# A two-layer graph network on one core: a head start for the second layer, its root term added early, and other groups at the end

## The chip, the cores and the metric

The kernel runs on one core of a Trainium2 chip. The metric is the device time of one execution in microseconds. Twenty executions of the kernel before had a median of 4745.5 us, from 4725.66 to 4767.5. One execution was profiled; it took 4727.98 us.

## The reference

There are N = 12500 nodes with C = 128 channels, and E = 200000 edges that are sorted by destination. Every edge has 42 attributes; the greatest of ten of them gives its relation. Two layers of a relational graph convolution follow, then a residual and a normalisation, all in 32-bit floating point:

```python
seg = dst * NUM_REL + edge_type
xs = x[src]
sums = jax.ops.segment_sum(xs, seg, num_segments=N * NUM_REL)
cnt = jax.ops.segment_sum(jnp.ones(seg.shape, x.dtype), seg, num_segments=N * NUM_REL)
mean = (sums / jnp.maximum(cnt, 1.0)[:, None]).reshape(N, NUM_REL, -1)
return jnp.einsum('nrd,rdo->no', mean, w_rel) + x @ root + bias
...
edge_type = jnp.argmax(msg[:, NODE_EMB_DIM:-NODE_EMB_DIM], axis=1).astype(jnp.int32)
h = jax.nn.relu(_rgcn_layer(x, src, dst, edge_type, w_rel1, root1, b1))
return _rgcn_layer(h, src, dst, edge_type, w_rel2, root2, b2)
...
x = _layernorm(x + _L0_gnn_ref(...), axis=-1)
```

So a layer needs, for each edge, the row of its source node; for each node, ten means over its incoming edges, each times its own 128 x 128 matrix; and the node's own row times a root matrix, plus a bias.

## The kernel before, in words

The edges are cut into 1563 tiles of 128 edges, and the tiles into groups: 95 groups of 16 tiles and then small ones, 8, 8, 8, 8, 4, 4 and 3 tiles. Both layers run over the groups in this order. The edges of a group lie within a short stretch of nodes, since they are sorted.

For each group these steps follow one another, and the steps of neighbouring groups overlap:

- POOL gathers the source rows of each tile with an indirect DMA (line 466) into one of three buffers g, from x in layer 1 and from hD, the hidden nodes in DRAM, in layer 2. One wait covers a whole group.
- DVE builds for each tile a matrix oh (line 481): an edge's weight (one over its count) in the column of its relation and its node's place among twelve.
- PE multiplies rows and oh into zp, sums by relation and node (line 495). There is one zp of four PSUM banks.
- ACT copies zp to zs (line 509), PE multiplies by the relations' matrices into pp (line 521), ACT copies to ms (line 527), PE spreads the result over 160 node columns with a placement matrix at (line 537), and DVE adds these to acc at an offset read from a register (line 543). acc has one column per node, and lies in SBUF for the whole time.

The weights of the edges need the relation and the counts of 13 chunks of 128 tiles (types() and count()). Chunk c+1 is prepared in steps while layer 1 runs over chunk c: the list todo holds, for each chunk, the group by which its steps are to be done and how many there are, and layer() runs some steps after each group.

A node block is finished as soon as no later group can touch it. There are 29 blocks: 23 of 512 nodes, five of 128 and one of 84. done_after() tells the tile after which a block is finished: blocks 23 to 28 fall into the small groups at the end. For a block, block_in() loads its rows of x (layer 2: also of hD), transposes the rows on PE (line 407) and copies them to fT (line 409). block_rows() adds the bias to the block's columns of acc (line 416), clears these columns in layer 1 (line 418), and multiplies fT by the root matrix and a by the identity into one PSUM tile (lines 421 and 422). In layer 1 hidden() applies relu (line 435) and stores the rows to hD. In layer 2 final() adds x (line 447), normalises (lines 450 to 457) and stores the rows to the output. The PSUM pool ps_f with its two buffers serves these steps and the counting.

Layer 2's first gather waits for all stores to hD. All direct DMAs of blocks and chunks are issued from SP. The order of instructions on an engine is given by a scheduler that works from the program order and its own estimates, except where keep_in_program_order fixes it.

After layer 2 a branch follows that is taken only where the data breaks an assumption of the fast path (a node with very many edges, for example); with these inputs it isn't taken.

Of the kernel before, what the change touches and what calls it, by code (L numbers as in the profile page):

```python
# [9 lines left out]
F32 = mybir.dt.float32  # L10
BF16 = mybir.dt.bfloat16
I32 = mybir.dt.int32
# [31 lines left out]
def rgcn_resnorm_kernel(ctx: ExitStack, tc: tile.TileContext, x, src, dst, attr, w_rel1, root1, b1,  # L44
# [25 lines left out]
    while t < NT:  # L70
        groups.append((t, min(HT if NT - t > 3 * QB else QB, NT - t)))
        t += groups[-1][1]
# [15 lines left out]

    HALF = NT * P - E
    assert C == P and E % GT == 0 and 0 < HALF < P and NT % CT and 1 < groups[-1][1] < groups[-2][1]  # L90

# [26 lines left out]
    wE = keep.tile([P, NCH * CT], F32, name="wE")  # L118

# [46 lines left out]

    def sources(c):
        p = chunk_rows(c)
        s_i = prep.tile([P, P], I32, name="s_i")
        rows_from(s_i, src, c, 0, P)  # L170
        s_f = prep.tile([P, P], F32, name="s_f")
        early(c, nc.vector.tensor_copy(s_f[:p], s_i[:p]))
        return to_edges(idxE, s_f, c)
# [112 lines left out]
    def types(c):  # L286
# [3 lines left out]
        d_i = prep.tile([P, P + L + 1], I32, name="d_i")  # L290
        if last:
            nc.vector.tensor_copy(d_i[:p, P:], pads[:p])
            q = p - 1
            nc.sync.dma_start(d_i[:q], bass.AP(dst.tensor, dst.offset + c * CE, [[P, q], [1, P + L + 1]]))
            nc.sync.dma_start(d_i[q:p, :P], bass.AP(dst.tensor, dst.offset + E - P, [[P, 1], [1, P]]))
        else:
            rows_from(d_i, dst, c, 0, P + L + 1)
        n = p - 1 if last else p
        ty = prep.tile([P, P], F32, name="ty")
        H = P // 2  # L300
        for o in (0, H):
            m = prep.tile([P, H * D], F32, name=f"m{o // H}")
            d = nc.sync.dma_start(m[:n], bass.AP(attr.tensor, attr.offset + (c * CE + o) * D, [[P * D, n], [1, H * D]]))
            if last:
                nc.sync.dma_start(m[n:p], bass.AP(attr.tensor, attr.offset + (E - P + o) * D,
                                                  [[P * D, 1], [1, H * D]]))
            if c == 1:
                later(d)
            argmax(c, ty[:p, o:o + H], m[:p].rearrange("p (j d) -> p j d", d=D)[:, :, EMB:EMB + NREL], p, H, prep,
                   riotaP, topP[o // H])  # L310
            yield
# [71 lines left out]
    def rows_dma(sb, dr, k, store):  # L383
        n0, n, _ = block(k)
        full = n // P
        pairs = []
        if full:
            pairs.append((sb[:, :full], dr[n0:n0 + full * P, :].rearrange("(t p) c -> p t c", p=P)))
        if n % P:
            pairs.append((sb[:n % P, full], dr[n0 + full * P:n0 + n, :]))  # L390
        for a, b in pairs:
            then("SP", nc.sync.dma_start(b, a) if store else nc.sync.dma_start(a, b))

    def block_in(k, l):

        n0, n, subs = block(k)
        last = "e" if k == NBLK - 1 else ""
        b = len(subs) if last else 4
        xb = fin.tile([P, b, C], F32, name="xb" + last)
        rows_dma(xb, x, k, False)  # L400
        fb = xb
        if l:
            fb = fin.tile([P, b, C], F32, name="hb" + last)
            rows_dma(fb, hD, k, False)
        pt = ps_f.tile([P, YB], F32, name="pf")
        for t, h in subs:
            nc.tensor.transpose(pt[:, t * P:t * P + h], fb[:h, t, :], ident[:h, :h])  # L407
        fT = fin.tile([P, b * P], F32, name="fT" + last)
        nc.scalar.activation(fT[:, :n], pt[:, :n], AF.Copy)  # L409
        return xb, fT  # L410

    def block_rows(fT, k, l):

        n0, n, subs = block(k)
        a = fin.tile([P, YB], F32, name="a")
        nc.vector.tensor_scalar(a[:, :n], acc[:, n0:n0 + n], bsb[l], None, op0=ALU.add)
        if l == 0:
            nc.vector.memset(acc[:, n0:n0 + n], 0.0)
        pr = ps_f.tile([P, 4, C], F32, name="pf")
        for t, h in subs:  # L420
            nc.tensor.matmul(pr[:h, t, :], fT[:, t * P:t * P + h], rsb[l], start=True, stop=False)  # L421
            nc.tensor.matmul(pr[:h, t, :], a[:, t * P:t * P + h], ident, start=False, stop=True)  # L422
        return pr
# [5 lines left out]
    def hidden(k, ready):  # L429

        xb, fT = ready
        pr = block_rows(fT, k, 0)
        hb = fin.tile([P, 4, C], F32, name="hb")
        for p, s in spans(k):
            nc.scalar.activation(hb[:p, s], pr[:p, s], AF.Relu)
        rows_dma(hb, hD, k, True)

    def final(k, ready):

        xb, fT = ready  # L440
        pr = block_rows(fT, k, 1)
        v = fin.tile([P, 4, C], F32, name="v")
        mv = small.tile([P, 4, 2], F32, name="mv")
        rstd = small.tile([P, 4], F32, name="rstd")
        _, n, subs = block(k)
        for p, s in spans(k):
            nc.vector.tensor_tensor(v[:p, s], pr[:p, s], xb[:p, s], op=ALU.add)  # L447
# [7 lines left out]
        o = fin.tile([P, 4, C], F32, name="o")  # L455
# [3 lines left out]
        rows_dma(o, out, k, True)  # L459
# [3 lines left out]

    def gather(table, t0, n):
        g = gpool.tile([P, G, C], F32, name="g")
        return g, [then("POOL", nc.gpsimd.indirect_dma_start(  # L466
            out=g[:, j, :], out_offset=None, in_=table, in_offset=bass.IndirectOffsetOnAxis(
                ap=idxE[:, t0 + j:t0 + j + 1], axis=0))) for j in range(n)]
# [6 lines left out]
    def ones(k):  # L475

        t0, n = groups[k]
        oh = dpool.tile([P, G, KW], F32, name="oh")
        for j in range(n):
            t = t0 + j  # L480
            then("DVE", nc.vector.tensor_scalar(oh[:, j, :], iotaP[:, :KW], keyE[:, t:t + 1], wE[:, t:t + 1],  # L481
                                                op0=ALU.is_equal, op1=ALU.mult))
# [3 lines left out]
        return oh, at  # L486

    def sums(table, k, oh, at):
# [4 lines left out]
        zp = ps_z.tile([P, G // QB, YB], F32, name="zp")  # L493
        for j in range(n) if end else reversed(range(n)):
            m = nc.tensor.matmul(zp[:, j // QB, j % QB * KW:(j % QB + 1) * KW], g[:, j, :], oh[:, j, :],  # L495
                                 start=True, stop=True)
# [48 lines left out]
    def layer(table, l, finish, steps, flag_too=False):  # L545
# [8 lines left out]
        def add_oldest():  # L554
# [3 lines left out]
            while done < NBLK and sum(groups[k]) >= done_after(done):  # L558
                finish(done, ready if done == NBLK - 1 else given or block_in(done, l))
# [3 lines left out]
        for k in range(NG):  # L563
            end = k >= NS
            if k and not given and done < NBLK - 1:
                given = block_in(done, l)
            if projected:
                add_oldest()
            if end:
# [4 lines left out]
                if not ready:  # L574
                    ready = block_in(NBLK - 1, l)
# [6 lines left out]
            held.append(sums(table, k, *(made or ones(k))))  # L582
            made = ones(k + 1) if end and k < NG - 1 else None
# [27 lines left out]
    zero = fin.tile([P, YB], F32, name="a")  # L611
    nc.vector.memset(zero, 0.0)
    for a in range(0, NPAD, YB):
        m = min(NPAD - a, YB)
        nc.scalar.activation(acc[:, a:a + m], zero[:, :m], AF.Copy)
# [3 lines left out]
    weights_in()  # L619
    todo = []  # L620
    for c in range(1, NCH):
        s = [as_steps(sources, c + 1)] if c + 1 < NCH else []
        todo.append((c * CT // G - 2, [8 + L // DB + 2], chain(*s, types(c), count(c))))
# [22 lines left out]

    gp = ctx.enter_context(tc.tile_pool(name="gp", bufs=2))
# [120 lines left out]
    with tc.If(flag > 0):  # L768
# [3 lines left out]
        for l, (table, finish) in enumerate(((x, hidden), (hD, final))):  # L772
            nc.vector.memset(acc, 0.0)
# [29 lines left out]
```

## Time and profile before

| | |
|---|---|
| median of 20 executions | 4745.5 us (4725.66 to 4767.5) |
| the profiled execution | 4727.98 us |
| its span, first to last instruction | 4726.2 us |
| granted TensorE clock in it | 0.746 |
| busy: POOL, PE, DVE, ACT | 63%, 58%, 32%, 11% of the span |
| start-up, until the first add to acc | 0 to 99 us |
| full groups of layer 1 | until 2284.6 us |
| small groups of layer 1 | until 2389.3 us |
| full groups of layer 2 | until 4617.5 us |
| small groups of layer 2 | until 4726.2 us |

A row of the timeline begins with the start in us and the length in us. After the operation stand the tiles, as output<-input, the shapes and the number of instructions that the row joins; in brackets the engine's idle time before it and what ended that. In the page's groups the columns after the bar are the busy time, the mean of one instruction in ns, and the idle time before them with its releaser. PE does each matmul of 32-bit numbers in two records. In the table by stage each engine's busy time and number of instructions are followed by the granted clock, the share of the DMA engines and GB/s.

### The profile page before, as it was taken

What the parts mean: (1) busy time and instruction counts of PE and PEld (TensorE: products, weight loads), DVE (VectorE), ACT (ScalarE), POOL (GpSimd) and SP (SyncE); (2) the same over time, 40 slices, a digit from 0 to 9 for tenths busy, and PEclk for the clock granted to TensorE, in tenths of its full rate; (3) what the DMA queues carried; (4) which work ended last, traced back from release to release, by engine and by line L of the source; (5) the groups of instructions that cost most, each with busy time, mean ns of one, the idle gap of its engine ahead of it and who ended that gap; (6) DMA issues with size and microseconds to landing.
All of it is one profiled execution on the core that took longest, in us unless ns stands there. A gap on an engine that the chain in (4) does not pass through costs nothing.

```text
span 4726.2 us, 43799 instructions
## 1 busy us (share of the span) xinstructions
PE 2759.9 (58%) x16206; PEld 2528.9 (54%) x16206; DVE 1511.0 (32%) x4660; ACT 530.9 (11%) x1142; POOL 2964.5 (63%) x3142
## 2 busy tenths in 40 slices
PE   2656566656656565655636556555556565665557
PEld 2545555555555555555625555555555555555556
DVE  4243333333334333333222322222222222222223
ACT  1010111111111111111101111111111111111111
POOL 5666666666666666666556666666666666666663
PEclk7777777777777777777766777777777777777778
DMA  4122222122122221211111111111111111111111
GB/s 132 48 72 79 62 63 80 49 76 74 55 76 62 63 77 49 57 49 49 45 48 48 55 52 52 56 55 52 52 56 55 52 50 57 54 52 52 57 53 39
DMA packets 180538, 278.99 MB, mean 59 GB/s; under 512 B 55608, under 2 KB 127175, under 8 KB 177191
## 3 DMA queue, kind: packets, MB, share of 16 engines
q0 software_dynamic: 100032, 205.07, 15.2%
q1 hardware_dynamic: 78577, 71.03, 4.7%
q8 instruction: 132, 2.16, 0.2%
q14 instruction: 89, 0.73, 0.0%
q10 hardware_dynamic: 1708, 0.01, 0.0%
HBM read 262.28 MB, written 13.60 MB: 58 GB/s over the span
## 4 chain that ended last, share of the span: by engine, by line
PE 36%; another core or an unknown queue 30%; issue 22%; DVE 10%; ACT 1%; DMA 0%; DVEq 0%; ACTq 0%
PE pp L521 17%; PE zp L495 12%; DVE oh L481 6%; PE pp L537 3%; PE pf L422 2%; PE pf L421 1%; ACT zs L509 1%; DVE at L485 1%; DVE acc L543 1%; PE pf L366 0%; PE pf L364 0%; PE pf L407 0%; DVE eqb L362 0%; DVE st L450 0%
## 5 line engine op out<-in xcount | busy, mean ns | idle before, releaser
L466 POOL DMA_INDIRECT g<-in_x_dram,idxE x1563 | 1481.2, 948 | 886.2 <-issue 428.3
L466 POOL DMA_INDIRECT g<-hD,idxE x1563 | 1480.6, 947 | 851.0 <-issue 453.3
L521 PE MATMUL pp<-w,zs 128*96 128x128 f32 x7880 | 1346.5, 336 | 702.1 <-issue 565.2
L521 PEld LDWEIGHTS pp<-w,zs 128*96 128x96 f32 x7880 | 1231.5, 212 | 823.8 <-issue 677.9
L495 PE MATMUL zp<-oh,g 128*128 128x120 f32 x6252 | 1030.9, 323 | 304.6 <-issue 267.3
L481 DVE TENSOR_SCALAR oh<-bank,keyE,wE 128x120 f32<-128x120 f32 x3126 | 1003.0, 391 | 570.4 <-remote 471.9
L495 PEld LDWEIGHTS zp<-oh,g 128*128 128x128 f32 x6252 | 981.0, 239 | 321.4 <-issue 299.0
L543 DVE TENSOR_TENSOR acc<-acc,pp 128x160 f32 x204 | 65.7, 322 | 1834.7 <-remote 1440.4
L509 ACT ACTIVATE zs<-zp 128x480 f32<-128x480 f32 (+1 forms) x782 | 385.6, 574 | 2172.6 <-remote 1606.6
L537 PE MATMUL pp<-at,ms 96*128 96x160 f32 (+1 forms) x788 | 208.1, 398 | 656.3 <-issue 545.9
L537 PEld LDWEIGHTS pp<-at,ms 96*128 96x128 f32 (+1 forms) x788 | 149.0, 241 | 699.7 <-issue 579.1
L527 ACT ACTIVATE ms<-pp 96x256 f32<-96x256 f32 (+1 forms) x198 | 74.5, 376 | 1310.7 <-remote 995.3
L422 PE MATMUL pf<-ident,a 128*128 128x128 f32 x392 | 116.8, 389 | 148.6 <-issue 73.6
L422 PEld LDWEIGHTS pf<-ident,a 128*128 128x128 f32 x392 | 90.7, 282 | 161.9 <-issue 81.5
L421 PE MATMUL pf<-root,fT 128*128 128x128 f32 x388 | 107.2, 366 | 70.0 <-issue 55.0
L362 DVE TENSOR_TENSOR eqb<-pf,kh 128x1344 bf16<-128x1344 f32 (+2 forms) x65 | 100.3, 1550 | 134.7 <-PE pp L537 74.4
L485 DVE TENSOR_SCALAR at<-bank,place 96x160 f32<-96x160 f32 x394 | 133.0, 371 | 0.0
L421 PEld LDWEIGHTS pf<-root,fT 128*128 128x128 f32 x388 | 86.7, 271 | 71.8 <-issue 55.4
L447 DVE TENSOR_TENSOR v<-pf,xb 128x512 f32<-128x512 f32 (+1 forms) x28 | 17.4, 620 | 219.4 <-remote 161.1
L369 DVE TENSOR_REDUCE wp<-pf 128x128 f32<-128x512 f32 (+2 forms) x13 | 9.0, 691 | 170.0 <-remote 155.2
L364 PE MATMUL pf<-eqb,identb 128*128 128x512 bf16 (+2 forms) x130 | 53.1, 409 | 15.7 <-DVE eqb L362 9.9
L409 ACT ACTIVATE fT<-pf 128x512 f32<-128x512 f32 (+1 forms) x56 | 30.3, 541 | 284.8 <-remote 239.7
(107 smaller groups left out, 484.4 us busy)
## 6 DMA issues: line engine op xcount, KB each, us to landing
m<-in_edge_attr_dram SPq DMA_DIRECT2D x24, 1344.0 KB
g<-in_x_dram,idxE POOLq DMA_INDIRECT x1563
g<-hD,idxE POOLq DMA_INDIRECT x1563
xb<-in_x_dram SPq DMA_DIRECT2D x46, 256.0 KB
hD<-hb SPq DMA_DIRECT2D x23, 256.0 KB
hb<-hD SPq DMA_DIRECT2D x23, 256.0 KB
out_dram<-o SPq DMA_DIRECT2D x23, 256.0 KB
w<-in_L_gnn_w_rel_dram SPq DMA_DIRECT2D x2, 640.0 KB
```

Source lines behind the costliest of these rows:

```text
L362: nc.vector.tensor_tensor(eq[:p], kp[:p, None, :R].to_broadcast([p, DB, R]), fore, op=ALU.is_equal)
L421: nc.tensor.matmul(pr[:h, t, :], fT[:, t * P:t * P + h], rsb[l], start=True, stop=False)
L422: nc.tensor.matmul(pr[:h, t, :], a[:, t * P:t * P + h], ident, start=False, stop=True)
L466: return g, [then("POOL", nc.gpsimd.indirect_dma_start(out=g[:, j, :], out_offset=None, in_=table, in_offset=bass.IndirectOffsetOnAxis(ap= ...
L481: then("DVE", nc.vector.tensor_scalar(oh[:, j, :], iotaP[:, :KW], keyE[:, t:t + 1], wE[:, t:t + 1], op0=ALU.is_equal, op1=ALU.mult))
L485: nc.vector.tensor_scalar(at[:, h, :], iotaP[:HR], place[:, h, k:k + 1], None, op0=ALU.is_equal)
L495: m = nc.tensor.matmul(zp[:, j // QB, j % QB * KW:(j % QB + 1) * KW], g[:, j, :], oh[:, j, :], start=True, stop=True)
L509: then("ACT", nc.scalar.activation(zs[:, :, b * QB:b * QB + m, :], zp[:, b, :m * KW].rearrange("c (j r n) -> c r j n", r=NREL, n=WN), AF.C ...
L521: nc.tensor.matmul(po[:m * WN, h], zs[:, r, h * HT:h * HT + m].rearrange("c j n -> c (j n)"), wsb[l][:, r, :], start=(r == 0), stop=(r == ...
L527: nc.scalar.activation(ms[:, :n // HT], po[:HR, :n // HT], AF.Copy)
L537: nc.tensor.matmul(pa, ms[:m * WN, h], at[:m * WN, h], start=(h == 0), stop=(h == len(parts) - 1))
L543: nc.vector.tensor_tensor(acc[:, s], acc[:, s], pa, op=ALU.add)
```

## The change

- **Groups.** The small groups at the end are 8, 8, 8, 12 and 7 tiles in place of 8, 8, 8, 8, 4, 4 and 3.
- **A head for layer 2.** The first 16 tiles of layer 2 gather from the first 12288 rows of hD alone, with indices held below 12288 (idxH). Edges whose source is one of the last 212 nodes get weight zero there (wH). Their part is added by late_sums(): matmuls of late_h, the rows of the last two blocks as they lie in SBUF, and late_w, which says for each of the last 212 nodes with what weight it goes to which column. head() builds late_w in five steps during the last full groups of layer 1, with a matmul per tile and block. The last chunk's preparation is to be done four groups earlier.
- **No nodes loaded in layer 2.** acc starts from layer 1's bias, set by ACT after the weights have come. hidden() transposes its rows in SBUF after relu, multiplies them by layer 2's root matrix (one matmul of up to 512 columns), and writes that, plus layer 2's bias, plus fT (the transposed rows of x) over the block's columns of acc. So final() only transposes acc into PSUM and normalises from there; block_in() does nothing in layer 2.
- **Shared transfers.** Sources and destinations of four chunks come in one DMA each; the attributes of a chunk in one instead of two; rows of x, hD and the output for two blocks of 512 nodes in one.

```diff
-        groups.append((t, min(HT if NT - t > 3 * QB else QB, NT - t)))
+        n = NT - t
+        groups.append((t, HT if n > 2 * HT + QB else HT + QB if n > HT + QB else n))
...
+    EARLY = starts[NBLK - 2]
...
+    def of_four(c, a, name, n):
+
+        if c == 0 or c == NCH - 1:
+            return prep.tile([P, n], I32, name=name)
+        if c % 4 == 1:
+            q = min(4, NCH - 1 - c)
+            four[name] = prep.tile([P, 4, n], I32, name=name + "4")
+            nc.sync.dma_start(four[name][:, :q], bass.AP(a.tensor, a.offset + c * CE, [[P, P], [CE, q], [1, n]]))
+        return four[name][:, (c - 1) % 4]
...
+        m = prep.tile([P, P * D], F32, name="m")
         for o in (0, H):
-            m = prep.tile([P, H * D], F32, name=f"m{o // H}")
-            d = nc.sync.dma_start(m[:n], bass.AP(attr.tensor, attr.offset + (c * CE + o) * D, [[P * D, n], [1, H * D]]))
...
+            w = H if c == 0 else P
+            if w == H or not o:
+                d = nc.sync.dma_start(m[:n, o * D:(o + w) * D], bass.AP(
+                    attr.tensor, attr.offset + (c * CE + o) * D, [[P * D, n], [1, w * D]]))
...
     def block_in(k, l):
 
+        if l:
+            return None
...
-        a = fin.tile([P, YB], F32, name="a")
-        nc.vector.tensor_scalar(a[:, :n], acc[:, n0:n0 + n], bsb[l], None, op0=ALU.add)
-        if l == 0:
-            nc.vector.memset(acc[:, n0:n0 + n], 0.0)
...
+    def hidden(k, fT):
+
+        n0, n, subs = block(k)
+        pr = ps_f.tile([P, 4, C], F32, name="pf")
+        for t, h in subs:
+            nc.tensor.matmul(pr[:h, t, :], fT[:, t * P:t * P + h], rsb[0], start=True, stop=False)
+            nc.tensor.matmul(pr[:h, t, :], acc[:, n0 + t * P:n0 + t * P + h], ident, start=False, stop=True)
+        i = k - (NBLK - 2)
+        hb = late_h[:, i:i + 1] if i >= 0 and not anew else half(k, "hb")
         for p, s in spans(k):
             nc.scalar.activation(hb[:p, s], pr[:p, s], AF.Relu)
-        rows_dma(hb, hD, k, True)
...
+        rows_dma(hb, hD, k, True, "hb")
+        pt = ps_f.tile([P, YB], F32, name="pf")
+        for t, h in subs:
+            nc.tensor.transpose(pt[:, t * P:t * P + h], hb[:h, t, :], ident[:h, :h])
+        hT = fin.tile([P, YB], F32, name="hT")
+        nc.scalar.activation(hT[:, :n], pt[:, :n], AF.Copy)
+        po = ps_f.tile([P, YB], F32, name="pf")
+        nc.tensor.matmul(po[:, :n], rsb[1], hT[:, :n], start=True, stop=True)
+        nc.vector.scalar_tensor_tensor(acc[:, n0:n0 + n], po[:, :n], bsb[1], fT[:, :n], op0=ALU.add, op1=ALU.add)
+
+    def final(k, _):
+
+        n0, n, subs = block(k)
+        v = ps_f.tile([P, 4, C], F32, name="pf")
...
+        for t, h in subs:
+            nc.tensor.matmul(v[:h, t, :], acc[:, n0 + t * P:n0 + t * P + h], ident, start=True, stop=True)
...
+    def head():
+
+        nc.vector.tensor_scalar(idxH, idxE[:, :G], EARLY - 1, None, op0=ALU.min)
...
+        for b in range(0, G, QB):
+            pm = [ps_f.tile([P, YB], F32, name="pf") for _ in range(2)]
+            for j in range(QB):
+                t = b + j
+                oh = prep.tile([P, KW], F32, name="ohH")
+                nc.vector.tensor_scalar(oh, iotaP[:, :KW], keyE[:, t:t + 1], wE[:, t:t + 1],
+                                        op0=ALU.is_equal, op1=ALU.mult)
+                for i in range(2):
+                    of = prep.tile([P, P], F32, name=f"of{i}")
+                    nc.vector.tensor_scalar(of, iotaP[:, :P], off[:, i, t:t + 1], None, op0=ALU.is_equal)
+                    nc.tensor.matmul(pm[i][:, j * KW:(j + 1) * KW], of, oh, start=True, stop=True)
+            for i in range(2):
+                nc.scalar.activation(late_w[i][:, b * KW:(b + QB) * KW], pm[i][:, :QB * KW], AF.Copy)
+            yield
...
+    def late_sums(table, t0, banks):
+
+        if is_head(table, t0):
+            for b, z in enumerate(banks):
+                for i in range(2):
+                    n = block(NBLK - 2 + i)[1]
+                    nc.tensor.matmul(z[:, :QB * KW], late_h[:n, i, :], late_w[i][:n, b * QB * KW:(b + 1) * QB * KW],
+                                     start=(i == 0), stop=False)
...
-    for a in range(0, NPAD, YB):
-        m = min(NPAD - a, YB)
-        nc.scalar.activation(acc[:, a:a + m], zero[:, :m], AF.Copy)
     places()
     for _ in chain(types(0), count(0)):
         pass
     weights_in()
+    for a in range(0, NPAD, YB):
+        m = min(NPAD - a, YB)
+        nc.scalar.activation(acc[:, a:a + m], zero[:, :m], AF.Identity, bias=bsb[0])
...
-        todo.append((c * CT // G - 2, [8 + L // DB + 2], chain(*s, types(c), count(c))))
+        todo.append((c * CT // G - (2 if s else 6), [8 + L // DB + 2], chain(*s, types(c), count(c))))
+    todo.append((NS - 1, [G // QB + 1], head()))
```

half() and rows_dma() give two neighbouring blocks of 512 nodes one buffer of twice the size and one transfer: a load is issued for the first of the two, a store with the second.

## The prediction

> **What bounds the kernel now.** I read the page first, then a table of busy time by stage, then the timeline around one node block and around the two ends of the layers.
>
> The page (columns: busy us, mean ns of one, then idle time before them and its releaser):
>
> ```profile
> L466 POOL DMA_INDIRECT g<-in_x_dram,idxE x1563 | 1481.2, 948 | 886.2 <-issue 428.3
> L466 POOL DMA_INDIRECT g<-hD,idxE x1563 | 1480.6, 947 | 851.0 <-issue 453.3
> L422 PE MATMUL pf<-ident,a 128*128 128x128 f32 x392 | 116.8, 389 | 148.6 <-issue 73.6
> L447 DVE TENSOR_TENSOR v<-pf,xb 128x512 f32<-128x512 f32 (+1 forms) x28 | 17.4, 620 | 219.4 <-remote 161.1
> ```
>
> POOL paces the kernel: 3126 gathers of 0.948 us and 0.30 us between them make 3908 of the span's 4726.2 us. The rest, 818 us, is pauses between groups. Only what shortens or lengthens a pause counts.
>
> By stage (start-up, full groups of layer 1, its end, full groups of layer 2, its end):
>
> ```profile
> 99.00:2284.60 2185.60, 1302.18 (x7619) 1178.29 (x7619) 779.80 (x2209) 241.13 (x511) 1380.51 (x1457) 0.74 0.21 63
> 2284.60:2389.30 104.70, 77.69 (x527) 71.71 (x527) 37.54 (x150) 18.13 (x47) 40.71 (x44) 0.84 0.14 39
> 2389.30:4617.50 2228.20, 1278.46 (x7433) 1190.37 (x7434) 623.63 (x2092) 236.04 (x506) 1439.89 (x1521) 0.74 0.19 53
> 4617.50:4726.20 108.70, 76.92 (x519) 70.29 (x517) 36.77 (x130) 18.11 (x47) 40.69 (x43) 0.85 0.14 39
> ```
>
> Each layer's last 43 tiles take 105 to 109 us, where 43 gathers at 1.25 us are 54. The 95 full groups of layer 2 take 23.45 us each, with 20.0 of gathers.
>
> A group of layer 1 with a node block, then the next group (timeline: start, length):
>
> ```profile
> 1271.85 0.32 DVE L543 TENSOR_TENSOR acc<-acc,pp 128x160 f32 x1 [5.53 <-remote]
> 1273.56 0.51 DVE L416 TENSOR_SCALAR a<-acc,b 128x512 f32<-128x512 f32 x1
> 1274.43 0.48 DVE L418 MEMSET acc<- 128x512 f32 x1
> 1274.86 0.95 POOL L466 DMA_INDIRECT g<-in_x_dram,idxE  x1 [0.30 <-issue]
> ...
> 1279.44 0.60 ACT L435 ACTIVATE hb<-pf 128x512 f32<-128x512 f32 x1 [17.18 <-PE pf L422]
> 1280.79 0.94 POOL L466 DMA_INDIRECT g<-in_x_dram,idxE  x1 [4.98 <-PE zp L495]
> ...
> 1302.87 0.32 DVE L543 TENSOR_TENSOR acc<-acc,pp 128x160 f32 x1 [10.34 <-remote]
> ...
> 1304.08 0.94 POOL L466 DMA_INDIRECT g<-in_x_dram,idxE  x1 [3.59 <-PE zp L495]
> ```
>
> POOL waits 3.45 to 3.6 us after a plain group, 4.98 us here: it needs the gather buffer of three groups ago, released by PE's zp. The next add to the accumulator comes 23 us after the relu.
>
> Between the layers:
>
> ```profile
> 2367.30 20.01 SPq L392 DMA_DIRECT2D hD<-hb  x3
> 2369.80 0.95 POOL L466 DMA_INDIRECT g<-in_x_dram,idxE  x1 [0.30 <-issue]
> 2385.40 0.32 DVE L543 TENSOR_TENSOR acc<-acc,pp 128x160 f32 x1 [1.22 <-PE pp L537]
> 2389.26 0.95 POOL L466 DMA_INDIRECT g<-hD,idxE  x1 [18.51 <-issue]
> ```
>
> POOL idles 18.5 us, until the last of the three stores that begin at 2367.30 (block 26) has landed.
>
> **The change part by part.** The sum is against the profiled execution, 4728.0 us (span 4726.2 and 1.8 around it), 17.5 us under the median of 4745.5; the difference is then put on the median.
>
> *Boundary: -14.* Layer 2's first 16 gathers (16 x 1.25 = 20.0 us) need only block 26. Its store is issued at 2367.3; I let it land 2 us later (the last store took from 2387.0 to 2389.3 until the gather) and add 2 us for the blocks' longer work: they run 2371 to 2391. Meanwhile the chain of adds must end. It had adds at 2371.6, 2376.3, 2381.1 and 2385.4; groups of 12 and 7 need two, each with some 2.4 us more of projection (20 records take 2.42 us) and 2 us for hidden's new steps: block 28 lands near 2386. The second group then starts at 2391 in place of 2409.3, -18. But PE is slow in the second half of a burst of 16 gathers (in a plain layer 2 group it did single matmuls between 3031 and 3041 us, and went on densely 3 us after the last gather). So I give back 4: -14. The late sums add 8 matmuls of 480 columns (40 records of L521, 128 columns each, took 4.53 us where PE is dense, 0.113 each; two records of 480 columns are 0.85, all 7 us) ahead of layer 2's first zp; three gather buffers, 60 us of gathers, cover them, and without that cover POOL's wait for the first zp, 7.6 us before the fourth group, grows by 7. Bounds: -20, all of it; and 0, if the 17.6 us from the last gather to the last store only begin when the burst is over (2391 + 17.6 = 2408.6).
>
> *End of layer 2: -13.* One chain step fewer after the last gather: -4.6 (adds at 4704.1 and 4708.8). Two groups fewer: their pauses of 3.0 and 1.2 us, of which I take -3. Six blocks finish here without loads, transposes (0.27 us), root matmul (0.46), a (0.29) and v (0.29): 0.9 each on PE and DVE, which are in line there (zp at 4668.0 waited for DVE's oh, queued behind a block's normalisation): -5.4. Bounds: -24 (each block 2 us, three steps of 4.6 less), 0 (layer 1's seven groups needed 86 us from first to last gather with lighter blocks, layer 2's 85: loads do not show).
>
> *Layer 2's other blocks: -9.* PE loses 16 of 24 records per block, DVE a (0.5) and v (0.62). Over plain groups a block costs some 0.8 us of pause, 22 x 0.8 = 18; half of it goes. Bounds: -18, 0.
>
> *Layer 1's blocks: +7.* Gone: a (0.51) and memset (0.48), and PE's wait for a. New after the relu: four transposes (0.60 us, as L407), an ACT copy (0.60), a matmul of 512 columns (eight such records, 0.9) and one DVE pass into acc from PSUM and SBUF (0.62, as v). The later steps have 23 us until the next add, so ACT and DVE hide them. PE does 1.5 us more and waits in order for relu and copy; behind it stand the remaining zp matmuls, which POOL's pause waits for. Some pf slots (two) are shared with counting. Net 0.3 us x 22 = +7. Bounds: 22 x -1 (the pause falls to a plain one) and 22 x +3 (relu and copy waited for with hops of 1.3 us each, and 0.5 of work) = -22 and +66.
>
> One rule speaks of the removed memset. While it ran at 1274.43, POOL's gathers kept their 1.25 us pitch (1273.61, 1274.86), so it is worth nothing to POOL. The Trainium skill (SBUF — State Buffer, SBUF: two separate sides) says that a DVE pass between fp32 tiles in SBUF in a two-port mode keeps GpSimd from writing descriptors; by it the removed passes, at most 29 x 0.9 = 26 us by the rows, would also be won, and the forecast would be some 4698. The row decides.
>
> *head(): +6.* 48 DVE passes of 0.39 us, 64 PE records of 0.27 and 8 ACT copies of 0.57, in five groups of layer 1: 3.7 us of DVE and 3.5 of PE per group beside 23 us. Its single buffers make DVE and PE alternate. I take 1 us for each of five groups, and 1 in all for the last chunk's closer steps. Bounds: 0, and 5 x 5 = 25 (group 88, with the last chunk's types, paused 5.8 us over a plain one).
>
> *Transfers and start: +2.* Attribute loads of 2.69 MB instead of two of 1.34 MB, and pairs of blocks, are issued groups ahead; fewer SP issues (0.33 us each) gain nothing, as SP is idle. The accumulator's 25 ACT passes (0.61 us each, from 11.7 us on) now follow the loads issued at 26.85 to 35, and ACT's first zs copy, at 79.8, is queued behind them; the 45 us between cover 15. Bounds: -3, +8.
>
> Sum: -14 -13 -9 +7 +6 +2 = -21: 4707 for the profiled execution, 4724 on the median.
>
> **The rivals.** (1) *Layer 1's chain lengthens each pause*: 3 us x 22 = 66 in place of 7: 4724 + 59 = 4783. For it: PE runs in order and its counters come late in bursts (the relu at 1279.44 began 0.5 us after PE's last pf matmul of 1278.92, but the next add came 14 us after its own matmul of 1288.4). Against: that same gap hides the new DVE pass. It decides from 1.3 us a block (28 us) on, where the gains are used up; slower shows from 1.7. (2) *The boundary or the loads were hidden anyway*: boundary 0 gives 4738; layer 2's blocks and finals 0 gives 4738 as well. For it: layer 2's blocks cost only 0.8 us. Against: 18.5 us of idle POOL. (3) *head() alternates DVE and PE at slow hops*: 32 exchanges of 1 us more, some 35 in place of 6: 4753. (4) *All pauses shrink*: layer 1 blocks -1 each, the others near their bounds: 4695.
>
> **How the numbers follow.** Chances: forecast 0.47, its own range 4705 to 4742; rival 1 0.22; rival 2 0.13; rival 3 0.08; rival 4 0.10. 0.2%, 9.5 us, is about what can be told from no change. Under 4736: most of the forecast (0.40), rival 4 (0.10), part of rival 2 (0.05): 0.55. Within: 0.06 + 0.07 + 0.04 + 0.02 = 0.19. Above 4755: 0.20 of rival 1, 0.04 of rival 3, 0.02 of others: 0.26. The range 4680 to 4788 leaves out the outer parts of rivals 1 and 4.
>
> **What would show it.** POOL's longest idle before a gather from hD falls from 18.5 us to under 3, and a second, shorter one appears before the second group; last gather to end shrinks from 23.8 us to about 19; layer 2's block groups pause like plain ones; layer 1's block groups stay near 24.8 us and the five with head() near 24. Wrong if layer 1's full groups take over 2225 us from 99 us on, if the tail's adds only come after the head's burst, or if DVE rows of head() show long waits for PE.

## The result and the profile after

The changed kernel took 4808.4 us (median of 7 runs, 4800.15 to 4815.28) against 4746.2 us of the kernel before (median of 47): a ratio of 1.0134, with a 95% interval of 1.0117 to 1.0151. It is 62 us slower where 21 us of gain were forecast. The profiled executions, 4809.5 and 4728.0 us, lie 82 us apart, since the one of before was 18 us under its median.

All runs of one set agree within 1%, but sets differ: in this comparison and three later sets POOL pauses some 3 us after every group, in four others it doesn't pause in the full groups, and the two kernels then take 3927 to 3948 us. The prediction and this result belong to the first condition; the second is told with the experiments.

The page of the changed kernel (busy us, mean ns of one, idle time before and its releaser). Gathers cost what they did, 0.944 us; POOL's idle time is longer in layer 1 (886 us before) and shorter in layer 2 (851 before), though 16 of layer 2's gathers now stand in a row of their own:

```profile
L536 POOL DMA_INDIRECT g<-in_x_dram,idxE x1563 | 1475.5, 944 | 989.4 <-issue 431.5
L536 POOL DMA_INDIRECT g<-hD,idxE x1547 | 1459.5, 943 | 814.0 <-issue 434.6
L462 PE MATMUL pf<-ident,acc 128*128 128x128 f32 x196 | 60.1, 402 | 64.0 <-issue 49.3
L475 DVE SCALAR_TENSOR_TENSOR acc<-pf,b,fT 128x512 f32<-128x512 f32 (+1 forms) x28 | 19.0, 679 | 182.8 <-PE pf L474 181.2
```

The table of busy time by stage, with the borders at the starts of groups: the 9th, the 91st and the 96th of layer 1, the second and the 96th of layer 2. After the borders stands the length, then busy time and instructions of PE, its weight loads, DVE, ACT and POOL. The kernel before:

```profile
0.00:207.20 207.20, 85.58 (x448) 68.48 (x449) 80.01 (x214) 26.68 (x54) 124.02 (x144) 0.73 0.30 95
207.20:2165.60 1958.40, 1169.57 (x6868) 1063.84 (x6868) 696.79 (x1976) 219.09 (x464) 1243.62 (x1313) 0.74 0.22 65
2165.60:2284.60 119.00, 71.67 (x417) 64.16 (x416) 36.29 (x104) 12.81 (x28) 75.61 (x80) 0.74 0.17 47
2284.60:2409.30 124.70, 80.69 (x537) 73.64 (x537) 41.78 (x163) 18.73 (x48) 55.83 (x60) 0.79 0.17 48
2409.30:4617.50 2208.20, 1275.46 (x7423) 1188.44 (x7424) 619.39 (x2078) 235.44 (x505) 1424.77 (x1505) 0.74 0.18 53
```

And the changed kernel:

```profile
0.00:203.70 203.70, 84.17 (x449) 65.86 (x450) 81.37 (x223) 28.99 (x54) 123.75 (x144) 0.74 0.31 98
203.70:2240.50 2036.80, 1208.43 (x6992) 1095.04 (x6992) 705.32 (x1951) 230.85 (x485) 1238.52 (x1312) 0.74 0.21 62
2240.50:2385.30 144.80, 86.96 (x503) 77.86 (x501) 39.35 (x114) 16.12 (x34) 75.48 (x81) 0.72 0.14 41
2385.30:2518.10 132.80, 85.26 (x522) 75.29 (x521) 51.09 (x187) 21.80 (x56) 55.63 (x60) 0.79 0.13 37
2518.10:4700.50 2182.40, 1303.71 (x7178) 1181.57 (x7177) 607.37 (x2037) 220.18 (x483) 1418.95 (x1505) 0.74 0.17 48
4700.50:4807.60 107.10, 68.58 (x468) 63.89 (x466) 32.34 (x113) 16.05 (x40) 40.51 (x43) 0.82 0.12 34
```

So the 81.4 us between the spans are: start -3.5, layer 1's groups 9 to 90 +78.4, the five groups with head() +25.8, layer 1's end and the border of the layers +8.1, layer 2's full groups -25.8, and its end -1.6 (107.1 against 108.7).

Most of the 78 us lies in the 21 of these groups in which the relu of a node block falls: they take 28.35 us each, where before they took 25.11, which makes 68 us. One of them (timeline of the changed kernel):

```profile
1211.00 0.32 DVE L625 TENSOR_TENSOR acc<-acc,pp 128x160 f32 x1 [3.92 <-remote]
...
1213.15 0.63 PE L462 MATMUL pf<-ident,acc 128*128 128x128 f32 x2
1213.57 1.90 PE L576 MATMUL zp<-oh,g 128*128 128x120 f32 x8
1223.13 0.60 ACT L466 ACTIVATE hb<-pf 128x512 f32<-128x512 f32 x1 [16.58 <-remote]
1223.78 1.12 PE L470 MATMUL pf<-ident,hb 128*128 128x128 f32 x4 [8.30 <-ACT hb L466]
1224.69 1.90 PE L576 MATMUL zp<-oh,g 128*128 128x120 f32 x8
1226.38 1.93 PE L474 MATMUL pf<-hT,root 128*128 128x512 f32 x2
1228.10 1.72 PE L576 MATMUL zp<-oh,g 128*128 128x120 f32 x8
1230.10 0.94 POOL L536 DMA_INDIRECT g<-in_x_dram,idxE  x1 [10.23 <-PE zp L576]
```

PE's record of the block's last matmul (a record is one instruction's entry in the trace) ends at 1213.8, but ACT begins the relu at 1223.1. That is 9.3 us later, and 3 us after POOL's last gather of the burst, as the back-to-back gathers of a group are called here (1218.9 to 1219.9, the start of POOL's idle time). The trace also has the times at which PE's semaphore moved: for this matmul at 1223.10, so the report was late and not ACT. In between PE stands 8.3 us at the transposes, which need the relu; 16 records of zp are queued behind them in two portions, and POOL's buffer is behind zp: a pause of 10.2 us. Before, in the block shown with the prediction, the relu also began 3.6 us after the burst (at 1279.44, POOL idle since 1275.81), though only 0.04 us after PE's last record for it. There a step ahead of it came late: the add at 1271.85, which the block's matmuls need, 7.9 us after PE's record of pp. And nothing that POOL needs stood in PE's queue behind that relu, since the rest of zp began before it:

```profile
1263.23 0.71 PE L537 MATMUL pp<-at,ms 96*128 96x160 f32 x4
...
1279.24 1.27 PE L495 MATMUL zp<-oh,g 128*128 128x120 f32 x10
```

At the border the head's gathers run from 2483.12 on, and then POOL waits again:

```profile
2480.69 0.32 SPq L430 DMA_DIRECT2D hD<-hb  x1
2483.12 0.94 POOL L536 DMA_INDIRECT g<-hD,idxH  x1 [14.81 <-PE zp L576]
2495.96 0.43 ACT L607 ACTIVATE ms<-pp 96x128 f32<-96x128 f32 x2 [11.74 <-remote]
2505.16 0.32 DVE L625 TENSOR_TENSOR acc<-acc,pp 128x160 f32 x1 [16.76 <-remote]
2518.10 0.94 POOL L536 DMA_INDIRECT g<-hD,idxE  x1 [15.32 <-DMA hD<-late_h]
```

The add that block 27 needs comes at 2505.2, 2.4 us after the burst's last gather (2502.8 is where POOL's wait of 15.32 begins). Two waits of 15 us stand where one of 18.5 stood.

### The profile page after: what moved, and what is told of

It is laid out like the page before. It is cut to its first block, busy times and chain, and to the rows that moved or that the text cites. A ratio compares the mean times of both kernels' runs of the same rounds, so it can differ in the third digit from the quotient of the medians.

```text
span 4807.6 us, 43310 instructions
## 1 busy us (share of the span) xinstructions
PE 2837.1 (59%) x16104; PEld 2559.5 (53%) x16104; DVE 1516.8 (32%) x4621; ACT 534.0 (11%) x1148; POOL 2952.8 (61%) x3142
## 4 chain that ended last, share of the span: by engine, by line
another core or an unknown queue 35%; PE 33%; issue 20%; DVE 10%; ACT 2%; DMA 0%; DVEq 0%; ACTq 0%
PE pp L603 17%; PE zp L576 11%; DVE oh L552 7%; PE pp L619 2%; ACT zs L591 1%; DVE at L556 1%; PE pf L474 1%; DVE eqb L385 1%; DVE acc L625 1%; PE pf L461 0%; PE pf L484 0%; PE pf L470 0%; PE pf L462 0%; PE pf L387 0%
## 5 line engine op out<-in xcount | busy, mean ns | idle before, releaser
L603 PE MATMUL pp<-w,zs 128*96 128x128 f32 x7840 | 1445.1, 345 | 948.5 <-issue 845.4
L603 PEld LDWEIGHTS pp<-w,zs 128*96 128x96 f32 x7840 | 1283.2, 218 | 1107.4 <-issue 999.0
L576 PE MATMUL zp<-oh,g 128*128 128x120 f32 x6252 | 1006.1, 324 | 120.6 <-issue 101.0
L619 PE MATMUL pp<-at,ms 96*128 96x160 f32 (+2 forms) x784 | 192.4, 375 | 498.3 <-issue 424.1
L619 PEld LDWEIGHTS pp<-at,ms 96*128 96x128 f32 (+2 forms) x784 | 136.7, 225 | 543.0 <-issue 460.9
L609 ACT ACTIVATE ms<-pp 96x256 f32<-96x256 f32 (+1 forms) x196 | 73.7, 376 | 1147.0 <-remote 823.6
L461 PE MATMUL pf<-root,fT 128*128 128x128 f32 x194 | 57.1, 389 | 90.6 <-DVE eqb L385 53.0
L487 DVE BATCH_NORM_STATS2 st<-pf 128x6 f32<-128x128 f32 x98 | 24.2, 286 | 252.1 <-remote 246.9
L462 PE MATMUL pf<-ident,acc 128*128 128x128 f32 x196 | 60.1, 402 | 64.0 <-issue 49.3
L461 PEld LDWEIGHTS pf<-root,fT 128*128 128x128 f32 x194 | 46.2, 289 | 94.5 <-DVE eqb L385 54.1
L484 PE MATMUL pf<-ident,acc 128*128 128x128 f32 x196 | 47.9, 416 | 75.6 <-issue 72.0
L462 PEld LDWEIGHTS pf<-ident,acc 128*128 128x128 f32 x196 | 48.1, 298 | 66.2 <-issue 50.6
L484 PEld LDWEIGHTS pf<-ident,acc 128*128 128x128 f32 x196 | 40.2, 301 | 80.7 <-issue 76.4
```

Source lines behind the costliest of these rows:

```text
L461: nc.tensor.matmul(pr[:h, t, :], fT[:, t * P:t * P + h], rsb[0], start=True, stop=False)
L462: nc.tensor.matmul(pr[:h, t, :], acc[:, n0 + t * P:n0 + t * P + h], ident, start=False, stop=True)
L484: nc.tensor.matmul(v[:h, t, :], acc[:, n0 + t * P:n0 + t * P + h], ident, start=True, stop=True)
L603: nc.tensor.matmul(po[:m * WN, h], zs[:, r, h * HT:h * HT + m].rearrange("c j n -> c (j n)"), wsb[l][:, r, :], start=(r == 0), stop=(r == ...
L619: nc.tensor.matmul(pa, ms[:m * WN, h], at[:m * WN, h], start=(h == 0), stop=(h == len(parts) - 1))
```

## The experiments

The first four undo or move one part each, all in one set; before took 4708.0 us there (median of 7), 38 us less than in the first comparison, and the changed kernel itself wasn't part of the set. The totals that were expected start from the first comparison, so the versions are compared by stages, with each other: one profile of each.

**The later steps of hidden() moved.** From the transposes on they are emitted behind the projection, with the first transpose pinned behind everything that PE has by then:

```diff
         rows_dma(hb, hD, k, True, "hb")
-        pt = ps_f.tile([P, YB], F32, name="pf")
-        ...
+        def second(pin=False):
+            pt = ps_f.tile([P, YB], F32, name="pf")
+            for t, h in subs:
+                m = nc.tensor.transpose(pt[:, t * P:t * P + h], hb[:h, t, :], ident[:h, :h])
+                if pin and not t:
+                    tc.keep_in_program_order(m)
+            ...
+        seconds.append(second) if full_group[0] else second()
...
             if end or len(held) > 1:
                 project_oldest()
+            while seconds:
+                seconds.pop(0)(True)
```

> The changed kernel with one thing moved: in layer 1's full groups hidden's transposes, copy, root matmul and pass into acc come in PE's order behind the group's zp and the projection, and no longer among the zp matmuls. Nothing is left out. Theory A (PE stands in order behind a relu that PE's own late counter holds up, with zp and so POOL's buffer behind it): the groups from the 9th to the 90th of layer 1, 78 us longer than before in the changed kernel, give back at least 45 us; about 4755 us in all. Rival B (the loss is the work itself, PE's 1.5 us per block, or the two PSUM buffers shared with counting): under 15 us come back, about 4795 to 4808.

Measured: 4741.8 us, ratio 1.0059 (1.0041 to 1.0078). Groups 9 to 90 of layer 1 took 1979.0 us, where the other three of this set, which keep the order, took 2017.5 to 2020.2. So 39 us come back from the order alone: B's "under 15" falls, A's "at least 45" wasn't reached. The timeline of a block's group in this version:

```profile
1184.68 2.51 PE L587 MATMUL zp<-oh,g 128*128 128x120 f32 x15
...
1192.54 0.60 ACT L466 ACTIVATE hb<-pf 128x512 f32<-128x512 f32 x1 [16.74 <-remote]
...
1194.31 0.94 POOL L547 DMA_INDIRECT g<-in_x_dram,idxE  x1 [4.94 <-PE zp L587]
...
1199.43 0.60 PE L472 MATMUL pf<-ident,hb 128*128 128x128 f32 x4
```

The relu is late as ever (PE's last record for it ends at 1184.9), but zp goes on without it and the pause of this group is 4.94 us, as before the change. Over all 21 groups with a block the mean is 25.7 us, against 27.8 in the three versions that keep the order.

**No head.** is_head() is always false, head() is not run, and the last chunk is due when it was before.

```diff
-        return table is hD and t0 < G
+        return False
...
-        todo.append((c * CT // G - (2 if s else 6), ...))
-    todo.append((NS - 1, [G // QB + 1], head()))
+        todo.append((c * CT // G - 2, ...))
```

> The changed kernel without the head: no head(), no late sums, layer 2's first group waits for all of hD like before, and the last chunk has its old due group. Theory A (head()'s single buffers make DVE and PE alternate over late counters, and the burst of the head's gathers holds up the last adds): the five groups with head() go from 145 us back to 119 to 124, and the stretch from the first small group of layer 1 to layer 2's second group from 133 to under 126; about 4775 us. Rival B (the head wins at the boundary what it costs before): the stretch grows by 15 us or more, and the total stays above 4795.

Measured: 4775.9 us, ratio 1.0136 (1.0112 to 1.0160). The five groups took 121.3 us (137.7 to 143.1 in the three others, which have the head), the stretch to layer 2's second group 127.8 (132.8 and 131.7 with the new groups and the head): A's 126 was just missed, B's longer stretch didn't come. Some 10 us of it are lost again in layer 2's full groups (2189.8 against 2179.9 and 2180.1 in the two versions with the head and the new groups; the excess lies in groups 2 to 5). The head costs where it is built, and in this condition doesn't shorten the border's stretch. A group in which it is built (changed kernel):

```profile
2342.78 0.40 DVE L521 TENSOR_SCALAR ohH<-bank,keyE,wE 128x120 f32<-128x120 f32 x1 [11.09 <-remote]
2343.49 0.78 PE L526 MATMUL pf<-ohH,of 128*128 128x120 f32 x2 [8.68 <-DVE of L525]
2354.91 0.94 POOL L536 DMA_INDIRECT g<-in_x_dram,idxE  x1 [15.27 <-PE pf L526]
```

DVE waits 11 us for PE to give its one buffer ohH back, PE then 8.7 us for DVE, and POOL 15.3 us for both.

**The small groups of before.**

```diff
-        n = NT - t
-        groups.append((t, HT if n > 2 * HT + QB else HT + QB if n > HT + QB else n))
+        groups.append((t, min(HT if NT - t > 3 * QB else QB, NT - t)))
```

> The changed kernel with the small groups of before, 8, 8, 8, 8, 4, 4 and 3. Theory A (a burst of 12 gathers is long enough for PE's counters to come late, a burst of 4 isn't): layer 2's small groups go from 107 us to 90 to 97 and layer 1's end is no longer; about 4795 us. Rival B (fewer groups save a chain step each, and what hurts the ends lies elsewhere): layer 2's small groups take 110 us or more; about 4815 us.

Measured: 4780.9 us, ratio 1.0150 (1.0133 to 1.0167). Layer 2's end took 98.7 us (107.1 to 110.4 with 12 and 7), and layer 1's end up to layer 2's second group 123.2 (131.7 to 132.8): 9 us each, A by its sign, though 98.7 is over its 97. What a burst of 12 does, in the changed kernel's last groups:

```profile
4757.70 0.60 PE L576 MATMUL zp<-oh,g 128*128 128x120 f32 x4
4767.61 1.03 ACT L591 ACTIVATE zs<-zp 128x480 f32<-128x480 f32 x2 [11.46 <-remote]
4767.79 0.94 POOL L536 DMA_INDIRECT g<-hD,idxE  x1 [2.65 <-remote]
```

PE's record of zp ends at 4758.3; ACT gets it 9.3 us later, when POOL has stood for 2.5 us. Three groups are then still to be added after the last gather, and 32.3 us pass from its start until the end where it was 24.7.

**Transfers of before.** Chunk by chunk, attributes in halves, blocks one by one (NPAIR = 0).

```diff
-    NPAIR = sum(b - a == YB for a, b in zip(starts, starts[1:])) // 2 * 2
+    NPAIR = 0
...
-        if c == 0 or c == NCH - 1:
-            return prep.tile([P, n], I32, name=name)
-        ...
-        return four[name][:, (c - 1) % 4]
+        return prep.tile([P, n], I32, name=name)
...
+            m = prep.tile([P, H * D], F32, name=f"m{o // H}")
+            d = nc.sync.dma_start(m[:n], bass.AP(attr.tensor, attr.offset + (c * CE + o) * D, [[P * D, n], [1, H * D]]))
```

> The changed kernel with the transfers of before: sources and destinations for one chunk, attributes in two halves, node blocks one by one. Theory A (transfers are issued long ahead and hidden either way): within 10 us of the changed kernel, 4798 to 4818. Rival B (one load of 2.69 MB into one buffer, or pairs that wait for their second block, are behind layer 1's longer groups at the chunk borders): 20 us or more faster, 4785 or less.

Measured: 4795.1 us, ratio 1.0180 (1.0163 to 1.0197). Layer 1's groups took 2018.1 us, as in the two versions with shared transfers and the same order. The total lies 3 us under A's range, in a set whose before is 38 us lower. By the stages B falls: the transfers are hidden either way.

**All together, and the kernels themselves.** The next set was to show whether the three mends add up (moved steps, no head, small groups of before), with before and the changed kernel beside it:

> The changed kernel with hidden's later steps behind the projection, without the head, and with the small groups of before; what is left of the change is that layer 2 loads no nodes, and the shared transfers. Theory A (order of PE's queue, head and groups account for the whole loss): the times by stage add up: layer 1's groups 9 to 90 some 20 us over before, layer 2's full groups 20 to 25 under it, the last small groups 10 under it: 10 us faster than before, ratio 0.996 to 1.000. Rival B (the moved root term costs layer 1 more than it saves in layer 2 wherever it stands): ratio over 1.004.

> The changed kernel, profiled and timed beside the others of this set, for its times by stage. If it keeps its distance to before, the ratio is 1.012 to 1.016; if the distance depends on the chip, up to 1.02.

> The kernel before, profiled on the chip of this set of runs, for its times by stage. The other set's before took 4708 us on another chip, the first 4746: if the stages differ in start-up or in layer 1 alone, a comparison by stages has to be made on one chip. Both theories expect 4700 to 4750 us.

It ran on the same chip some ten minutes later, and no kernel of it paused. The table has the time by stage, from the starts of gathers:

| us | before | changed | three mends |
|---|---|---|---|
| until layer 1's 9th group | 165.0 | 165.0 | 164.8 |
| groups 9 to 90 | 1641.1 | 1639.7 | 1639.3 |
| groups 91 to 95 | 99.9 | 99.9 | 99.9 |
| to layer 2's second group | 84.1 | 73.7 | 86.1 |
| layer 2's full groups from there | 1878.3 | 1877.9 | 1877.4 |
| layer 2's end | 75.8 | 69.4 | 72.9 |
| median, all runs of the set | 3946.6 | 3927.0 | 3942.7 |

The changed kernel is faster here, ratio 0.9948 (0.9933 to 0.9964): every full group takes 20.0 us of gathers whatever stands beside it, and the ends give 10.4 and 6.4 us. The three mends give most of that away with 0.9991 (0.9982 to 1.0000); that this lies in the range of theory A is luck, since no stage is as it said. The border of the layers in the changed kernel, with the same lines as above:

```profile
1944.58 0.32 SPq L430 DMA_DIRECT2D hD<-hb  x1
1958.26 0.95 POOL L536 DMA_INDIRECT g<-hD,idxH  x1 [0.30 <-issue]
1967.19 0.32 DVE L625 TENSOR_TENSOR acc<-acc,pp 128x160 f32 x1 [0.57 <-PE pp L619]
...
1976.99 0.94 POOL L536 DMA_INDIRECT g<-hD,idxH  x1 [0.30 <-issue]
```

The adds come while the head's gathers run, and POOL doesn't wait at all. Half of the mends, the moved steps and the old groups with the head kept, was tried in the same condition:

> As the version before it, but with the head. Where POOL pauses: the head's cost of some 20 us in layer 1 stays, ratio 1.002 to 1.007. Where it doesn't: the head hides the wait between the layers, some 10 us of gain, ratio 0.996 to 0.998.

3929.6 us, ratio 0.9955 (0.9942 to 0.9969), just under the 0.996 to 0.998 expected: the head brings 12.5 us (73.6 to layer 2's second group), the groups of 12 and 7 another 3.5 (69.4 against 72.9 at the end). Before and the three mends stood beside it in that set:

> The kernel before, profiled on this chip for its times by stage. Where POOL pauses: 4700 to 4750 us with layer 1's groups 9 to 90 in 1930 to 1960; where it doesn't, 3946 us with 1641.

> The version with hidden's later steps behind the projection, no head and the small groups of before, once more. In the set where POOL makes no pauses (before 3946 us) it had a ratio of 0.999. If POOL pauses after every group here (before near 4710 to 4750 us), theory A adds the stages up to a ratio of 0.996 to 1.000, rival B (the moved root term costs more than it saves wherever it stands) to over 1.004. If POOL makes no pauses here either, 0.999 again.

Before took 3947.95 us with the stages of the table's first column (1641.3 and 1878.3 for the full groups), the three mends 3942.9 us, ratio 0.9988 (0.9979 to 0.9997). Twice more the mended version was to run in the condition with pauses, and met the other:

> The version with hidden's later steps behind the projection, no head and the small groups of before. Where POOL pauses after each group (before at 4700 to 4750 us): by the stages of the single mends 0.996 to 1.000 of before; by rival B over 1.004. Where it makes no pauses (before near 3947 us): 0.999.

> The version with the three mends, again for the condition in which POOL pauses after each group (before at 4700 to 4750 us). There theory A expects a ratio of 0.996 to 1.000, rival B over 1.004. Without pauses (before near 3947 us) 0.999 as in the sets before.

3942.6 us, 0.9989 (0.9979 to 0.9998), and 3942.9 us, 0.9989 (0.9980 to 0.9999): neither says anything on whether the mends add up where POOL pauses.

**The condition with pauses once more.** It was back in two later sets, on other chips (before 4631.8 and 4630.0 us).

> The changed kernel with hidden's later steps behind the projection, and nothing else mended. Without pauses (before near 3947 us) PE's queue has room and the place of these steps is worth nothing: 3925 to 3929 us, ratio 0.994 to 0.9955 like the changed kernel. With pauses (before at 4700 to 4750 us) the ratio is 1.004 to 1.008 as in the first set.

4684.4 us, ratio 1.0117 (1.0100 to 1.0134): outside the 1.004 to 1.008 expected and worse than the 1.0059 of the first set, though layer 1's groups 9 to 90 were shorter (1936.1 us), as before's total was.

> The version with the three mends (later steps behind the projection, no head, the small groups of before), in the condition with pauses, if it still holds (before at 4630 to 4750 us). Theory A adds the stages of the single mends up to a ratio of 0.996 to 1.003; rival B (the moved root term costs layer 1 more than it saves in layer 2) to over 1.004.

4655.7 us, ratio 1.0064 (1.0047 to 1.0081). By its ratio rival B stands: even with the three mends, what is left of the change loses some 26 us where POOL pauses. That layer 1's blocks lose them isn't shown: the mended version's groups 9 to 90 took 1935.2 us, 45 more than 82 plain groups of its 23.05 us, and before's, in its one profile with pauses, took 53 more than 82 of its own 23.24. Nor does the ratio refute that the mends add up, for the moved steps alone lost 53 us to before in the other of these two sets and 34 in the first. No profile of before exists from the later sets, and where the 26 us lie stays open.

**Fewer PE instructions.** The changed kernel with five of the ten relations projected:

```diff
-            for r in range(NREL):
+            for r in range(0, NREL, 2):
                 nc.tensor.matmul(po[:m * WN, h], zs[:, r, ...], wsb[l][:, r, :],
-                                 start=(r == 0), stop=(r == NREL - 1))
+                                 start=(r == 0), stop=(r == NREL - 2))
```

It ran four times, and three of the sets had no pauses:

> The changed kernel with the projection by five of the ten relations only (the messages of the other five are left out), 20 PE records less per group of 16 tiles. Theory S (PE's late hand-over in a burst comes from the number of PE instructions that have to get through while POOL gathers): the plain pause of 3.1 us falls under 2 and the groups with a block under 25 us. Theory A' (PE's results are handed over late whenever POOL gathers for more than some 10 us, however little PE does): the plain pause stays at 3.1 us and layer 1's block groups stay over 26.5 us.

> The changed kernel with five of ten relations projected (the other five messages are left out), once more, since the last set showed no pauses in any kernel. Where before pauses: theory S (number of PE instructions) has the plain pause under 2 us and layer 1's block groups under 25 us; theory A' (PE's hand-overs are late under gathers, however little PE does) has the plain pause at 3.1 us and block groups over 26.5.

> The changed kernel with five of ten relations projected (the other five messages are left out). Where before pauses: theory S (number of PE instructions) has a plain pause under 2 us and layer 1's block groups under 25 us; theory A' (hand-overs are late under gathers however little PE does) 3.1 us and over 26.5 us.

These took 3923.1, 3922.4 and 3923.0 us. Without pauses there is nothing for fewer instructions to shorten, and they could not tell the theories apart. The fourth had them:

> The changed kernel with five of ten relations projected (the other five messages are left out), in the condition with pauses, if it still holds. Theory S (number of PE instructions): plain pause under 2 us and layer 1's block groups under 25 us. Theory A' (hand-overs late under gathers however little PE does): 3.1 us and over 26.5 us.

With pauses it took 4698.9 us in one run (before 4630.0 beside it), with 12184 PE records in place of 16104. The plain pause is 2.9 us, so S, which said under 2, falls. Layer 1's groups with a block fit neither theory as it was put: nine of the 21 take 37 to 41 us, each behind a group of 20.0 us without any pause, so that 32 gathers ran back to back, and the other twelve take 22 to 23.4, like plain ones. One of the long ones:

```profile
1145.11 2.35 PE L603 MATMUL pp<-w,zs 128*96 128x128 f32 x20
1150.31 1.96 ACT L591 ACTIVATE zs<-zp 128x480 f32<-128x480 f32 x4 [11.96 <-remote]
...
1181.13 0.38 ACT L609 ACTIVATE ms<-pp 96x256 f32<-96x256 f32 x1 [28.86 <-remote]
1181.56 1.43 PE L619 MATMUL pp<-at,ms 96*128 96x160 f32 x4 [34.11 <-ACT ms L609]
1183.03 0.32 DVE L625 TENSOR_TENSOR acc<-acc,pp 128x160 f32 x1 [36.69 <-PE pp L619]
1194.39 0.94 POOL L536 DMA_INDIRECT g<-in_x_dram,idxE  x1 [18.44 <-PE zp L576]
```

PE had nothing to do for 34 us but wait for ACT's copy; ACT waited for PE's own pp, whose record ends at 1147.5, and got it 33.7 us later, 5.2 us after POOL's last gather (POOL's idle time begins at 1175.95). So this hand-over didn't wait for work of PE. It came only after the burst; zp's, to ACT at 1150.31, came in the middle of the same burst.

## Why the prediction was wrong

The forecast needed every term, and by the stages of the profiles these are theirs. Its signs of being wrong came too: layer 1's full groups took 2286 us from 99 us on, over the 2225 it named, the last adds came after the head's burst, and DVE waited 11 us for PE in head().

- **Layer 1's blocks, +7 forecast, +78 measured, over the bound of +66.** This is the step that failed. "Relu and copy waited for with hops of 1.3 us each" was its highest price for a hand-over from PE; in the block shown the relu came 9.3 us after PE's record. What said so stood in the prediction: the add that came 14 us after its own matmul, which rival 1 named and the forecast took for cover, and PE's slow stretch between 3031 and 3041, used for the border alone. "The later steps have 23 us until the next add" was right for DVE and beside the point: PE stands in order, and zp is behind it. Rival 1 named this mechanism, at 3 us a block; the 21 groups with a block grew by 3.2 each. Moving the steps gave back 39 us, and what makes up the rest of the stage no run takes apart.
- **head(), +6 forecast, +26 measured.** The alternation of rival 3, but in the group shown not as many hops of 1 us: one exchange that fell into the second half of a burst held DVE for 11 us. Leaving the head out, with the last chunk due as before, gave 16 to 22 us in these groups.
- **Boundary, -14 forecast, +8 with layer 1's end measured.** The bound of 0, that the last adds come when the burst is over, is what happened (2505.2). The rest came with the groups of 12 and 7: with the small groups of before this stretch took 123.2 us, about as long as before the change (124.7, in the first comparison).
- **End of layer 2, -13 forecast, -1.6 measured.** PE's results came late in a burst of 12, which no term had: the stretch from the last gather to the end grew from 23.8 to 31.4 us, where 19 was foreseen. The small groups of before are worth 9 us here and 9 at layer 1's end.
- **Layer 2's blocks, -9 forecast, -26 measured**, beyond the bound of -18. Its blocks do pause like plain groups now (23.2 us). Some 9 us are two groups that were long in the profile of before alone (29.9 and 25.2 us); why they were, no run shows, and that part is luck.
- **Transfers and start, +2 forecast, -3.5 measured**: hidden, as said. The removed memset was worth nothing to POOL by its pitch, which stayed at 1.25 us a gather; no run takes the memset out alone.

Three slips in its working change nothing in this: from the last gather to the last store are 17.2 us by the rows and not 17.6, the lower bound of layer 2's end adds up to -26 and not -24, and PE loses 12 of 20 records per block of layer 2, since a transpose is one record.

Without pauses the sum of -21 would have had the right size (-19.6 us by the medians), by luck in part: the border gave -10.4 and the end -6.4, nearly as argued, but the blocks of either layer gave nothing, as their pauses aren't there.

## What to carry to other kernels

Here a step that waited for another engine's answer cost 39 us where it stood in PE's queue ahead of the work that releases POOL, and it is worth looking for such places in other kernels. Price such a wait by the latest hand-over that the profile shows in the same stretch, not by the shortest. And profile the kernel before beside each set of experiments: here the same program took 3947 us in some and 4630 to 4746 in others, and the changed kernel is slower than before in the one (1.0134) and faster in the other (0.9948).

## What the runs showed of the hardware

In the condition with pauses PE's results reach the other engines late while POOL issues gathers back to back. It isn't that nothing gets through before POOL stops: the add at 1211.00 came in the middle of a burst, 3.6 us after PE's record. But what PE finishes in the second half of a burst mostly arrives after it: 9.3 us late in bursts of 12 and of 16 gathers, 33.7 us late in one of 32 in the version with half the projections, where PE was idle. The trace of the changed kernel has 227 matmuls that report to another engine and end later than 10 us into a burst of 16; for 142 of them PE's semaphore next moves only after the burst, by the median 3.2 us after its end. For reports in the first 10 us it moves 2.9 us (median) after the record, and in the pauses 0.01 us.

In the other condition it moves after 0.01 us (median) in and out of bursts, and layer 1's blocks, the head and groups of 12 cost POOL nothing. Where PE runs densely its pace is the same in both (40 records in 4.53 us), and so is that of the gathers (1.25 us from one to the next). One chip showed both conditions within ten minutes, so the program and the chip don't decide which it is. What does, and what holds the reports up, no run tells.
